# A graph layer on one core: every source row gathered by GpSimd, fewer waits on TensorE, two node blocks a transfer

## The chip, the core and the metric

The kernel runs on one core of a Trainium2 chip. Its time is the device time of the run in microseconds. The core has TensorE (PE; PEld is its weight load), VectorE (DVE), ScalarE (ACT), GpSimd (POOL) and SyncE (SP), which work through their own instruction queues and wait for each other by semaphores. In this kernel POOL, SP and ACT also issue DMAs.

## What is computed

50000 nodes have 160 features: 64 scalars and 32 vectors of three. 1650000 edges, sorted by destination, carry four attributes each. Every edge's message is bilinear in the source node's row and the four attributes; messages are summed per destination, pass a linear layer and a ReLU, and are normalised with two residual additions:

```python
edge_index = jnp.stack([src, dst])
s, v = x[:, :64], x[:, 64:].reshape(n, 32, 3)
ss, vv = s[src], v[src]
e0, e1 = sh[:, 0:1], sh[:, 1:4]
dot  = jnp.einsum('eui,ei->eu', vv, e1)
out0 = C0 * (ss * e0 @ W1 + dot * INV3 @ W2)
p3   = (ss @ W3)[:, :, None] * e1[:, None, :] * INV3
p4   = jnp.einsum('eui,uw->ewi', vv * e0[:, :, None], W4) * INV3
p5   = jnp.einsum('eui,uw->ewi', jnp.cross(vv, e1[:, None, :]), W5) * INV6
out1 = C1 * (p3 + p4 + p5)
m_agg = segment_sum(concat(out0, out1), dst)
h     = concat(m_agg_s @ Ws * LIN_S, m_agg_v @ Wv * LIN_V)
x     = layernorm(x + (x + relu(h)))
```

The last 50000 edges made by the setup are self loops, one per node; after the sort each stands among the edges of its node.

## The kernel before

**Edges.** Since the message is linear in the source row, rows are summed first and multiplied by weights afterwards. Edges are taken 128 at a time (a unit); six units (G) make a group whose destinations fall in a window of 32 nodes (W); two groups make a pair (PG = 2), which is the step of the main loop, 1044 pairs in all. For each unit of a pair POOL gathers 128 rows of x by an indirect DMA into one slice of the tile `xg` (line 319, `gather`). Four `xg` buffers exist (pool "rows"), so POOL can fill the next pairs while PE reads an older one. VectorE makes the one-hot of the destinations (`hot`, line 328) and multiplies it by the four attributes (`ha`, line 331, `spread`); PE multiplies `ha` by the gathered rows and adds up six units in PSUM (`ps`, line 343, `group_sums`; two buffers); VectorE transposes the sums (line 349). Every two pairs make a chunk of four groups. Its sums are multiplied by the weights (`phc`, line 579, `apply_weights`) and copied to SBUF by ScalarE (`hp`, line 581).

**Rows fetched singly.** `HELP = {ET.SP: 72}`: once in 72 units the rows of one unit are not gathered by POOL. SP reads 128 offsets from `ro` (made by ScalarE, line 274) and issues one DMA per row into the tile `xr` (lines 671 to 677, `fetch`, in four batches of 32 over the pairs before). That unit is the last of its pair, and POOL then issues 11 gathers for the pair in place of 12.

**Nodes.** Blocks of 128 nodes (391) follow behind the chunks that they need. `ahead` (lines 588 to 597) issues the DMAs for a block's own rows `xt` and self-loop attributes `sa`; `own` turns `xt` by TensorE (`ptx`, line 615), has ScalarE copy it (`xT`, line 617), multiplies it by the weights (`yx`, line 623) and adds the four products on VectorE into `t` (lines 627, 629); `block` sums the chunks into the nodes (`phb`, line 639) and adds `t` (line 640); `norm1` (184 to 188), `norm2` (line 193, ScalarE) and `norm3` (197, 199) normalise; `do_send` issues the DMA to the output (line 735).

**Packs.** The self loops are taken out of the edge list on the chip beforehand. Rows of 790 edges are worked on 128 at a time (16 packs, each due every 65.8 pairs or so): read (lines 419 to 423), cast by ScalarE (427 to 429), scanned and shifted by VectorE in strides of 1 to 16 (`shift`, lines 504 to 511), and written by SP to the tables `edges` and `selves` row by row (`store`, `put`, line 563). A pack is a list of small steps, some of them empty; the main loop runs as many steps after each pair as spread the list evenly up to the pair at which the pack is due.

**Order.** The main loop calls these parts in the order of the pairs, with `after_pair(p, ...)` for what belongs behind pair p. A scheduler arranges the instructions of PE, VectorE, ScalarE and POOL from that; within the main loop SP keeps the program's order (line 799). Semaphore waits come from a dependency tracker, except for the one that is set by hand: the first product of a pair waits for all of the pair's gathers (lines 346 to 348).

Of the kernel before, what the change touches and what calls it, by code (L numbers as in the profile page):

```python
# [38 lines left out]
F32 = mybir.dt.float32  # L39
# [6 lines left out]
ET = mybir.EngineType  # L46
# [3 lines left out]
P = 128  # L50
MUL0, MUL1 = 64, 32
D = MUL0 + 3 * MUL1
NK = 4
# [9 lines left out]
W = 32  # L63
QG = P // W
FB = P // NK
ND = D // FB
PG = 2
SG = 20

HELP = {ET.SP: 72}  # L70
HEAD = 100
RP = 128
RS = 16
KM = 31
# [29 lines left out]
def tile_gnn_resnorm(ctx: ExitStack, tc: tile.TileContext, x, src, dst, attr, W1, W2, W3, W4, W5, Ws, Wv, out, n_edges):  # L104
# [86 lines left out]
    def norm2(pool, mv, n):  # L191
        rstd = pool.tile([P, 1], F32, name="rstd")
        nc.scalar.activation(rstd[:n], mv[:n, 1:2], AF.Sqrt, bias=eps_t[:n])  # L193
        return rstd

    def norm3(pool, y, mv, rstd, n):
        nc.vector.reciprocal(rstd[:n], rstd[:n])
        o = pool.tile([P, D], F32, name="o")
        nc.vector.tensor_scalar(o[:n], y[:n], mv[:n, 0:1], rstd[:n], op0=ALU.subtract, op1=ALU.mult)  # L199
        return o  # L200

# [23 lines left out]
    with tc.tile_pool(name="once", bufs=1) as once, tc.tile_pool(name="raw", bufs=2) as rawp, \  # L225
# [1 line left out]
            tc.tile_pool(name="far", bufs=3) as farp, \  # L227
            tc.tile_pool(name="ops", bufs=3) as op, tc.tile_pool(name="sums", bufs=4) as sump, \
            tc.tile_pool(name="hp", bufs=alive + 4) as hpp, tc.tile_pool(name="node", bufs=3) as np_, \
            tc.tile_pool(name="ahead", bufs=7) as aheadp, \  # L230
# [93 lines left out]
        def spread(placed, u, n):  # L324
# [8 lines left out]
                                    .to_broadcast([P, n, NK, W]), op=ALU.mult)  # L333
            return ha

        def group_sums(p, rows, ha, at, i):


            s, g0, ng = pairs[p]
            ps = psA.tile([P, PG, D], F32, name="ps")  # L340
            rows, got = rows
            for j, xr in enumerate(rows):
                mm = nc.tensor.matmul(ps[:, j // G, :], ha[:, j].rearrange("p k w -> p (k w)"), xr,  # L343
                                      start=j % G == 0, stop=j % G == G - 1)

                if j == 0 and p + 1 < len(pairs):
                    for r in got[1:]:
                        tc.add_manual_dep(mm.ins, r.name, LANDED)
            nc.vector.transpose(at[:, :, i:i + ng, :].rearrange("p b g w -> p g b w"),  # L349
                                ps[:, :ng].rearrange("p g (b f) -> p g b f", f=FB))  # L350
# [57 lines left out]
        def pack(c):  # L408
# [160 lines left out]


            for head, j in [(False, j) for j in range(RS)] + [(True, 0)]:
                steps += [partial(store, head, j), None, None, None]
            return steps + [stored]

        def apply_weights(at, ng):

            ph = psM.tile([P, D], F32, name="phc", tag="misc")
            for b in range(ND):
                nc.tensor.matmul(ph[:ng * W], at[:, b, :ng].rearrange("p g w -> p (g w)"), BWk[:, b, :], start=b == 0, stop=b == ND - 1)  # L579
            hp = hpp.tile([P, D], F32, name="hp")  # L580
            evict(hp[:ng * W], ph[:ng * W])  # L581
            return hp, ng * W

        def rows_of(b):
            nb = min(P, N - b * P)
            return nb, slice(b * P, b * P + nb)

        def ahead(b):

            nb, row = rows_of(b)  # L590
            xt = aheadp.tile([P, D], F32, name="xt")
            dq.dma_start(xt[:nb], x[row, :])

            assert rows_stored[0] == NR or row_start(rows_stored[0])[1][0] >= row.stop
            sa = aheadp.tile([P, NK], F32, name="sa")
            dq.dma_start(sa[:nb], selves[0, row.start * NK:row.stop * NK].rearrange("(n k) -> n k", k=NK))
            return xt, sa

        def nodes(b):

# [5 lines left out]
                                    rr[:, :len(cs)].unsqueeze(2).to_broadcast([P, len(cs), P]), op=ALU.is_equal)  # L606
            return hot2

        def own(b, xt, sa):

            nb, row = rows_of(b)
            H = D // 2
            pt = psM.tile([H, 2, P], F32, name="ptx", tag="misc")
            for i in range(2):
                nc.tensor.transpose(pt[:, i, :nb], xt[:nb, i * H:(i + 1) * H], ident[:nb, :nb])  # L615
            xT = np_.tile([H, 2, P], F32, name="xT")
            evict(xT[:, :, :nb], pt[:, :, :nb])  # L617
            t = aheadp.tile([P, D], F32, name="t")
            for h in range(NK // 2):
                y = psM.tile([P, 2, D], F32, name="yx", tag="misc")  # L620
                ks = slice(2 * h, 2 * h + 2)
                for i in range(2):
                    nc.tensor.matmul(y[:nb], xT[:, i, :nb], BWh[:, i, ks, :], start=i == 0, stop=i == 1)  # L623
                for i in range(2):
                    k = 2 * h + i
                    if k == 0:
                        nc.vector.tensor_scalar(t[:nb], y[:nb, i], sa[:nb, 0:1], None, op0=ALU.mult)  # L627
                    else:
                        nc.vector.scalar_tensor_tensor(t[:nb], y[:nb, i], sa[:nb, k:k + 1], t[:nb],  # L629
                                                       op0=ALU.mult, op1=ALU.add)  # L630
            return xt, t

        def block(b, xt, t, hot2):
            nb, row = rows_of(b)
            cs = of_block[b]
            ph = psM.tile([P, D], F32, name="phb", tag="misc")
            for i, c in enumerate(cs):
                hp, r = hps[c]
                nc.tensor.matmul(ph[:nb], hot2[:r, i, :nb], hp[:r], start=i == 0, stop=i == len(cs) - 1)  # L639
# [8 lines left out]
        for h, (eng, period) in enumerate(HELP.items()):  # L648
            first = PG * G + h * period // 2
            nbatch = P // ROWS[eng]  # L650
            while True:
                at = [int(first + i * period / nbatch) // (PG * G) for i in range(nbatch)]
                q = at[-1] + 2
                if q >= len(pairs) or pairs[q][2] < PG:
# [50 lines left out]

        later = {}

        def after_pair(p, f, *args):
            later.setdefault(p, []).append((f, args))

# [5 lines left out]
                of_nodes[b] += (nodes(b),)  # L716

        def do_ahead(b):
            of_nodes[b] = ahead(b)

        def do_own(b):
            of_nodes[b] = own(b, *of_nodes.pop(b))
# [5 lines left out]
            rstds[b] = norm2(np_, resid[b][1], rows_of(b)[0])  # L728

        def do_store(b):  # L730
            outs[b] = norm3(np_, *resid.pop(b), rstds.pop(b), rows_of(b)[0])

        def do_send(b):
            nb, row = rows_of(b)
            dq.dma_start(out[row, :], outs.pop(b)[:nb])

        def do_cast(s):
            raws[s] = cast(raws[s])
# [8 lines left out]
        def examine_all():  # L747
# [20 lines left out]
            bad = once.tile([P, 1], F32, name="bad")  # L768
            nc.vector.tensor_reduce(bad, wrong, axis=AX.X, op=ALU.max)
            pb = psM.tile([1, 1], F32, name="pb", tag="misc")  # L770
            nc.tensor.matmul(pb, bad, ones[:, 0:1], start=True, stop=True)
            nc.vector.tensor_scalar(more[:, 0:1], pb, 1.0, None, op0=ALU.min)
            nc.vector.tensor_scalar(more[:, 1:2], pb, 1.0, float(NB), op0=ALU.min, op1=ALU.mult)
# [21 lines left out]
        for at, bs in zip(complete, after):  # L795
            for b in bs:
                after_pair(max(at - AHEAD, START - 1), do_ahead, b)
                after_pair(max(at - AHEAD + 4, START), do_own, b)
        later_pools.enter_context(tc.manual_schedule(engines={ET.SP}))
        for p, (s, g, ng) in enumerate(pairs):  # L800
            if p % per == 0 and s + 1 < NSC:
# [116 lines left out]
    with tc.tile_pool(name="edges2", bufs=2) as ep, tc.tile_pool(name="ops2", bufs=2) as op, \  # L918
            tc.tile_pool(name="node2", bufs=1) as np_, tc.tile_pool(name="psA2", bufs=2, space=PSUM) as psA, \
            tc.tile_pool(name="psF2", bufs=1, space=PSUM) as psF:  # L920
        with tc.For_i(0, blocks, 1) as b:
# [52 lines left out]
            o = norm3(np_, y, mv, norm2(np_, mv, NBLK), NBLK)  # L974
            nc.scalar.dma_start(out[row, :], o[:NBLK])


# [31 lines left out]
```

## Time and profile before

| | |
|---|---|
| median of 5 runs | 15680.33 us (15676.18 to 15682.88) |
| the profiled execution: its own time, its span | 15677.19 us, 15675.4 us |
| busy | POOL 75%, PE 51%, PEld 46%, DVE 40%, ACT 3% |
| PE's granted clock (mean) | 0.739 |
| gathers on POOL (line 319) | 12349 |
| single-row DMAs on SP (line 676) | 22144 |
| HBM traffic over the span | 77 GB/s |

A group line gives engine, operation, what is written and read, the count, then busy time and mean ns of one, and after the second bar the idle time just ahead of the group with what ended it. A line of the waits reads: engine and line, what was waited for, then us in total, how often, and the longest. In the timeline the columns are start and duration in us, then the instruction; in brackets the idle time before it and what ended it. A line of stretches gives, after the window and its length, busy us and count of PE, PEld, DVE, ACT and POOL, then the granted clock, the DMA engines' share and GB/s. A line of the chain gives start, us and what.

### The profile page before, as it was taken

Reading aid. Unit: us, or ns where it says so; the run is one execution under the profiler, and the core shown is the slowest. Engines: PE = TensorE matmul, PEld = TensorE weight load, DVE = VectorE, ACT = ScalarE, POOL = GpSimd, SP = SyncE. Lnnn points to the kernel's source line nnn. Section 1 sums busy time; section 2 is a strip of 40 time slices with the busy share of each in tenths; the row PEclk is TensorE's granted clock in tenths of the full one; section 3 lists DMA queues with packets and bytes.
Section 4 is the critical chain, followed back from the end, with each engine's and each line's share of the span. In section 5 each row is a group of like instructions: output and inputs, shape, how many; then the busy total and the mean of one; then the engine's idle time right before and its main releaser. Section 6 shows DMA issues by size and latency. Waiting matters only on the chain. (4 is left out here: it accounts for less than half of the span.)

```text
span 15675.4 us, 167279 instructions
## 1 busy us (share of the span) xinstructions
PE 7993.0 (51%) x38505; PEld 7261.9 (46%) x38506; DVE 6237.9 (40%) x11070; ACT 537.8 (3%) x1497; POOL 11701.9 (75%) x12363
## 2 busy tenths in 40 slices
PE   4554545555555455454554444555555554555555
PEld 3444444444444444444444444444444444444444
DVE  5342525225253442524435243352433525234322
ACT  0000000000000000000000000000000000000000
POOL 7777777777777777777777777777777777777776
PEclk7777777777777777777777777777777777777777
DMA  3323232232232322323223232322323233232222
GB/s 80 86 73 83 71 79 78 77 85 73 78 80 78 82 73 79 80 78 83 72 79 79 78 82 74 83 73 77 82 76 82 74 79 79 78 80 72 77 73 66
DMA packets 843237, 1218.89 MB, mean 78 GB/s; under 512 B 300227, under 2 KB 623912, under 8 KB 838262
## 3 DMA queue, kind: packets, MB, share of 16 engines
q0 software_dynamic: 592752, 1012.42, 25.1%
q1 hardware_dynamic: 248058, 194.45, 4.3%
q8 instruction: 323, 5.29, 0.1%
q14 instruction: 664, 5.44, 0.1%
q10 hardware_dynamic: 1440, 1.29, 0.0%
HBM read 1135.77 MB, written 71.40 MB: 77 GB/s over the span
## 5 line engine op out<-in xcount | busy, mean ns | idle before, releaser
L319 POOL DMA_INDIRECT xg<-in_x,si x12349 | 11697.7, 947 | 3929.2 <-issue 3714.8
L343 PE MATMUL ps<-xg,ha 128*128 128x160 f32 x24698 | 5301.9, 392 | 6216.4 <-DMA xg<-in_x,si 5311.8
L343 PEld LDWEIGHTS ps<-xg,ha 128*128 128x128 f32 x24698 | 5066.7, 267 | 6439.0 <-issue 5551.3
L349 DVE STREAM_TRANSPOSE sums<-ps 128x320 f32<-128x320 f32 x1044 | 535.4, 513 | 6044.6 <-PE ps L343 5966.1
L331 DVE TENSOR_TENSOR ha<-hot,pk 128x1536 f32<-128x1536 f32 x1044 | 1801.2, 1726 | 722.3 <-PE ps L343 722.2
L579 PE MATMUL phc<-BWk,sums 128*128 128x160 f32 x5220 | 927.0, 331 | 784.7 <-DVE sums L349 678.2
L579 PEld LDWEIGHTS phc<-BWk,sums 128*128 128x128 f32 x5220 | 829.1, 211 | 860.5 <-DVE sums L349 721.1
L623 PE MATMUL yx<-BWh,xT 80*128 80x320 f32 x3128 | 1001.7, 466 | 175.9 <-ACT xT L617 175.0
L627 DVE TENSOR_SCALAR t<-yx,sa 128x160 f32<-128x160 f32 x391 | 149.4, 382 | 1834.6 <-PE yx L623 1824.0
L623 PEld LDWEIGHTS yx<-BWh,xT 80*128 80x128 f32 x3128 | 596.0, 200 | 469.5 <-ACT xT L617 263.0
L639 PE MATMUL phb<-hp,hot 128*128 128x160 f32 x3474 | 605.3, 323 | 300.6 <-DVE t L629 299.8
L639 PEld LDWEIGHTS phb<-hp,hot 128*128 128x128 f32 x3474 | 536.9, 206 | 397.2 <-issue 390.3
L328 DVE TENSOR_TENSOR hot<-bank,rel 128x384 f32<-128x384 f32 x1044 | 553.9, 545 | 4.0
L629 DVE SCALAR_TENSOR_TENSOR t<-yx,sa,t 128x160 f32<-128x160 f32 x1173 | 447.9, 382 | 133.0 <-PE yx L623 107.1
L617 ACT COPY xT<-ptx 80x256 f32<-80x256 f32 x391 | 143.8, 368 | 10391.6 <-PE ptx L615 10083.4
L511 DVE COPY_PREDICATED prow<-marks,prow 128x2370 f32<-128x2370 int32 (+8 forms) x160 | 443.4, 2771 | 0.6
L511 DVE COPY_PREDICATED pra<-marks,pra 128x1580 f32<-128x1580 int32 (+8 forms) x160 | 304.8, 1905 | 0.0
L605 DVE TENSOR_TENSOR hot<-bank,rr 128x512 f32<-128x512 f32 (+2 forms) x391 | 287.9, 736 | 0.0
L640 DVE TENSOR_TENSOR phb<-phb,t 128x160 f32<-128x160 f32 x391 | 129.6, 332 | 360.2 <-PE phb L639 357.6
L581 ACT COPY hp<-phc 128x160 f32<-128x160 f32 x522 | 150.2, 288 | 2909.7 <-PE phc L579 2853.8
L193 ACT ACTIVATE rstd<-mv,eps_t 128x1 f32<-128x1 f32 x391 | 115.2, 295 | 1734.1 <-DVE mv L188 1696.1
L615 PE MATMUL ptx<-ident,xt 128*80 128x128 f32 (+1 forms) x782 | 158.9, 287 | 0.0
(148 smaller groups left out, 2848.9 us busy)
## 6 DMA issues: line engine op xcount, KB each, us to landing
xr<-in_x SPq DMA_DIRECT2D x22144, 0.6 KB
xg<-in_x,si POOLq DMA_INDIRECT x12349
edges<-prow SPq DMA_DIRECT2D x1994, 18.5 KB
r<-edges SPq DMA_DIRECT2D x99, 360.0 KB
selves<-mine SPq DMA_DIRECT2D x1992, 0.5 KB
xt<-in_x SPq DMA_DIRECT2D x390, 80.0 KB
out<-o SPq DMA_DIRECT2D x390, 80.0 KB
pra<-in_attr SPq DMA_DIRECT2D x15, 1580.0 KB
```

The lines of the kernel that those rows point to most:

```text
L319: got.append(nc.gpsimd.indirect_dma_start(out=xg[:, j, :], out_offset=None, in_=x, in_offset=bass.IndirectOffsetOnAxis(ap=placed[0][:, u + ...
L328: nc.vector.tensor_tensor(hot[:, :n], slotsP[:, 0:W].unsqueeze(1).to_broadcast([P, n, W]), rel[:, u:u + n].unsqueeze(2).to_broadcast([P, n ...
L331: nc.vector.tensor_tensor(ha[:, :n], hot[:, :n].unsqueeze(2).to_broadcast([P, n, NK, W]), pk[:, :, u:u + n].rearrange("p k u -> p u k").un ...
L343: mm = nc.tensor.matmul(ps[:, j // G, :], ha[:, j].rearrange("p k w -> p (k w)"), xr, start=j % G == 0, stop=j % G == G - 1)
L349: nc.vector.transpose(at[:, :, i:i + ng, :].rearrange("p b g w -> p g b w"), ps[:, :ng].rearrange("p g (b f) -> p g b f", f=FB))
L511: nc.vector.copy_predicated(what[:n, a:e], mi[:, r].unsqueeze(2).to_broadcast([n, e - a, what.shape[2]]), what[:n, a + d:e + d])
L579: nc.tensor.matmul(ph[:ng * W], at[:, b, :ng].rearrange("p g w -> p (g w)"), BWk[:, b, :], start=b == 0, stop=b == ND - 1)
L605: nc.vector.tensor_tensor(hot2[:, :len(cs)], slotsP.unsqueeze(1).to_broadcast([P, len(cs), P]), rr[:, :len(cs)].unsqueeze(2).to_broadcast( ...
L615: nc.tensor.transpose(pt[:, i, :nb], xt[:nb, i * H:(i + 1) * H], ident[:nb, :nb])
L623: nc.tensor.matmul(y[:nb], xT[:, i, :nb], BWh[:, i, ks, :], start=i == 0, stop=i == 1)
L629: nc.vector.scalar_tensor_tensor(t[:nb], y[:nb, i], sa[:nb, k:k + 1], t[:nb], op0=ALU.mult, op1=ALU.add)
L639: nc.tensor.matmul(ph[:nb], hot2[:r, i, :nb], hp[:r], start=i == 0, stop=i == len(cs) - 1)
```

## The change

- `HELP` is empty: nothing is fetched singly, POOL gathers all units. ScalarE's offsets (`ro`) are no longer made.
- `wrote` and `fresh` keep a list of the PE instructions that wrote each PSUM slot of the tags "misc" and "ps". A write to a slot that two later ones have followed is declared independent of the slot's earlier writers on PE.
- `made` collects ScalarE's copies (`hp`, `xT`) by pair; the first product of pair p waits for those of pair p - 1.
- `own` is divided: `turned` (transposes of `xt` and the copy) is called three pairs after `ahead`, `own` five pairs after; before, all of it was called four pairs after.
- Two neighbouring blocks share one DMA for `xt`, one for `sa` and one for the output (`BP = 2`, `together`). Pool "ahead" has five buffers in place of seven, now of two blocks for `xt` and `sa`; `o` has three of two blocks.
- A pack's store steps are no longer followed by three empty ones.

```diff
-HELP = {ET.SP: 72}
+HELP = {}
+BP = 2
@@ group_sums
+        written = {"misc": [], "ps": []}
+        def fresh(kind):
+            written[kind].append([])
+        def wrote(kind, ins):
+            ws = written[kind]
+            for old in ws[-3] if len(ws) > 2 else []:
+                tc.declare_no_dep(ins.ins, old, reason="its reader has waited for it")
+            ws[-1].append(ins.ins)
+            return ins
...
+                if j % G == 0:
+                    wrote("ps", mm)
+                else:
+                    written["ps"][-1].append(mm.ins)
                 if j == 0 and p + 1 < len(pairs):
-                    for r in got[1:]:
+                    for r in got[1:] + made.pop(p - 1, []):
                         tc.add_manual_dep(mm.ins, r.name, LANDED)
@@ pack
             for head, j in [(False, j) for j in range(RS)] + [(True, 0)]:
-                steps += [partial(store, head, j), None, None, None]
+                steps.append(partial(store, head, j))
@@ apply_weights
-            evict(hp[:ng * W], ph[:ng * W])
+            made.setdefault(now[0], []).append(evict(hp[:ng * W], ph[:ng * W]).ins)
@@ ahead
-        def ahead(b):
+        def together(b):
+            bs = list(range(b // BP * BP, min(nblocks, b // BP * BP + BP)))
+            return bs if all(rows_of(i)[0] == P for i in bs) else [b]
+        def ahead(bs):
...
-            xt = aheadp.tile([P, D], F32, name="xt")
-            dq.dma_start(xt[:nb], x[row, :])
+            xt = aheadp.tile([P, BP, D], F32, name="xt")
+            dq.dma_start(xt[:nb, :len(bs)], x[n0:n1, :].rearrange("(h n) d -> n h d", h=len(bs)))
...
@@ own
-        def own(b, xt, sa):
+        def turned(b, xt, sa):
...
+            made.setdefault(now[0], []).append(evict(xT[:, :, :nb], pt[:, :, :nb]).ins)
+            return xt, sa, xT
+        def own(b, xt, sa, xT):
...
@@ do_send
-            dq.dma_start(out[row, :], outs.pop(b)[:nb])
+            bs = together(b)
+            if b == bs[-1]:
+                n0, n1 = rows_of(bs[0])[1].start, rows_of(b)[1].stop
+                dq.dma_start(out[n0:n1, :].rearrange("(h n) d -> n h d", h=len(bs)),
+                             outs.pop(bs[0])[:rows_of(b)[0], :len(bs)])
@@ main loop
-                after_pair(max(at - AHEAD + 4, START), do_own, b)
+                after_pair(max(at - AHEAD + 3, START), do_turned, b)
+                after_pair(max(at - AHEAD + 5, START + 2), do_own, b)
```

More of the change, by code (lines that the diff above doesn't have):

```diff
@@ L194, in norm2, with norm3 @@
         return rstd
-    def norm3(pool, y, mv, rstd, n):
+    def norm3(o, y, mv, rstd, n):
         nc.vector.reciprocal(rstd[:n], rstd[:n])
-        o = pool.tile([P, D], F32, name="o")
         nc.vector.tensor_scalar(o[:n], y[:n], mv[:n, 0:1], rstd[:n], op0=ALU.subtract, op1=ALU.mult)
@@ L229, in tile_gnn_resnorm @@
             tc.tile_pool(name="hp", bufs=alive + 4) as hpp, tc.tile_pool(name="node", bufs=3) as np_, \
-            tc.tile_pool(name="ahead", bufs=7) as aheadp, \
+            tc.tile_pool(name="ahead", bufs=5) as aheadp, tc.tile_pool(name="outs", bufs=3) as outp, \
             tc.tile_pool(name="psC", bufs=1, space=PSUM) as psC, tc.tile_pool(name="psK", bufs=2, space=PSUM) as psK, \
@@ L340, in group_sums @@
             ps = psA.tile([P, PG, D], F32, name="ps")
+            fresh("ps")
             rows, got = rows
@@ L577, in apply_weights @@
             ph = psM.tile([P, D], F32, name="phc", tag="misc")
+            fresh("misc")
             for b in range(ND):
-                nc.tensor.matmul(ph[:ng * W], at[:, b, :ng].rearrange("p g w -> p (g w)"), BWk[:, b, :], start=b == 0, stop=b == ND - 1)
+                wrote("misc", nc.tensor.matmul(ph[:ng * W], at[:, b, :ng].rearrange("p g w -> p (g w)"), BWk[:, b, :],
+                                               start=b == 0, stop=b == ND - 1))
             hp = hpp.tile([P, D], F32, name="hp")
-            evict(hp[:ng * W], ph[:ng * W])
+            made.setdefault(now[0], []).append(evict(hp[:ng * W], ph[:ng * W]).ins)
             return hp, ng * W
@@ L586, in rows_of @@
             return nb, slice(b * P, b * P + nb)
-        def ahead(b):
-            nb, row = rows_of(b)
-            xt = aheadp.tile([P, D], F32, name="xt")
-            dq.dma_start(xt[:nb], x[row, :])
[L594 to L597, printed above, removed]
+        def together(b):
+            bs = list(range(b // BP * BP, min(nblocks, b // BP * BP + BP)))
+            return bs if all(rows_of(i)[0] == P for i in bs) else [b]
+        def ahead(bs):
+            nb = rows_of(bs[0])[0]
+            n0, n1 = rows_of(bs[0])[1].start, rows_of(bs[-1])[1].stop
+            xt = aheadp.tile([P, BP, D], F32, name="xt")
+            dq.dma_start(xt[:nb, :len(bs)], x[n0:n1, :].rearrange("(h n) d -> n h d", h=len(bs)))
+            assert rows_stored[0] == NR or row_start(rows_stored[0])[1][0] >= n1
+            sa = aheadp.tile([P, BP, NK], F32, name="sa")
+            dq.dma_start(sa[:nb, :len(bs)],
+                         selves[0, n0 * NK:n1 * NK].rearrange("(h n k) -> n h k", h=len(bs), k=NK))
+            return [(xt[:, h], sa[:, h]) for h in range(len(bs))]
         def nodes(b):
@@ L607, in nodes @@
             return hot2
-        def own(b, xt, sa):
+        H = D // 2
+        def turned(b, xt, sa):
             nb, row = rows_of(b)
-            H = D // 2
             pt = psM.tile([H, 2, P], F32, name="ptx", tag="misc")
+            fresh("misc")
             for i in range(2):
-                nc.tensor.transpose(pt[:, i, :nb], xt[:nb, i * H:(i + 1) * H], ident[:nb, :nb])
+                wrote("misc", nc.tensor.transpose(pt[:, i, :nb], xt[:nb, i * H:(i + 1) * H], ident[:nb, :nb]))
             xT = np_.tile([H, 2, P], F32, name="xT")
-            evict(xT[:, :, :nb], pt[:, :, :nb])
+            made.setdefault(now[0], []).append(evict(xT[:, :, :nb], pt[:, :, :nb]).ins)
+            return xt, sa, xT
+        def own(b, xt, sa, xT):
+            nb, row = rows_of(b)
             t = aheadp.tile([P, D], F32, name="t")
@@ L620, in own @@
                 y = psM.tile([P, 2, D], F32, name="yx", tag="misc")
+                fresh("misc")
                 ks = slice(2 * h, 2 * h + 2)
                 for i in range(2):
-                    nc.tensor.matmul(y[:nb], xT[:, i, :nb], BWh[:, i, ks, :], start=i == 0, stop=i == 1)
+                    wrote("misc", nc.tensor.matmul(y[:nb], xT[:, i, :nb], BWh[:, i, ks, :], start=i == 0, stop=i == 1))
                 for i in range(2):
@@ L636, in block @@
             ph = psM.tile([P, D], F32, name="phb", tag="misc")
+            fresh("misc")
             for i, c in enumerate(cs):
                 hp, r = hps[c]
-                nc.tensor.matmul(ph[:nb], hot2[:r, i, :nb], hp[:r], start=i == 0, stop=i == len(cs) - 1)
+                wrote("misc", nc.tensor.matmul(ph[:nb], hot2[:r, i, :nb], hp[:r], start=i == 0, stop=i == len(cs) - 1))
             nc.vector.tensor_tensor(ph[:nb], ph[:nb], t[:nb], op=ALU.add)
@@ L653, in tile_gnn_resnorm @@
                 q = at[-1] + 2
-                if q >= len(pairs) or pairs[q][2] < PG:
+                if q >= len(pairs) - 10:
                     break
@@ L706, in tile_gnn_resnorm @@
         later = {}
+        now, made = [0], {}
         def after_pair(p, f, *args):
@@ L718, in do_ahead, with do_turned @@
         def do_ahead(b):
-            of_nodes[b] = ahead(b)
+            bs = together(b)
+            if b == bs[0]:
+                of_nodes.update(zip(bs, ahead(bs)))
+        def do_turned(b):
+            of_nodes[b] = turned(b, *of_nodes.pop(b))
         def do_own(b):
@@ L730, in do_store @@
         def do_store(b):
-            outs[b] = norm3(np_, *resid.pop(b), rstds.pop(b), rows_of(b)[0])
+            bs = together(b)
+            if b == bs[0]:
+                outs[b] = outp.tile([P, BP, D], F32, name="o")
+            norm3(outs[bs[0]][:, b - bs[0]], *resid.pop(b), rstds.pop(b), rows_of(b)[0])
         def do_send(b):
-            nb, row = rows_of(b)
-            dq.dma_start(out[row, :], outs.pop(b)[:nb])
+            bs = together(b)
+            if b == bs[-1]:
+                n0, n1 = rows_of(bs[0])[1].start, rows_of(b)[1].stop
+                dq.dma_start(out[n0:n1, :].rearrange("(h n) d -> n h d", h=len(bs)),
+                             outs.pop(bs[0])[:rows_of(b)[0], :len(bs)])
         def do_cast(s):
@@ L770, in examine_all @@
             pb = psM.tile([1, 1], F32, name="pb", tag="misc")
+            fresh("misc")
             nc.tensor.matmul(pb, bad, ones[:, 0:1], start=True, stop=True)
@@ L797, in tile_gnn_resnorm @@
                 after_pair(max(at - AHEAD, START - 1), do_ahead, b)
-                after_pair(max(at - AHEAD + 4, START), do_own, b)
+                after_pair(max(at - AHEAD + 3, START), do_turned, b)
+                after_pair(max(at - AHEAD + 5, START + 2), do_own, b)
         later_pools.enter_context(tc.manual_schedule(engines={ET.SP}))
         for p, (s, g, ng) in enumerate(pairs):
+            now[0] = p
             if p % per == 0 and s + 1 < NSC:
@@ L973, in tile_gnn_resnorm @@
             y, mv = norm1(np_, ph, xt, NBLK)
-            o = norm3(np_, y, mv, norm2(np_, mv, NBLK), NBLK)
+            o = np_.tile([P, D], F32, name="o")
+            norm3(o, y, mv, norm2(np_, mv, NBLK), NBLK)
             nc.scalar.dma_start(out[row, :], o[:NBLK])
```

## The prediction

> **What bounds the kernel now.** I read the busy line first, then the costliest groups, the waits of each engine, the timeline around the longest waits, stretches by engine, and the chain that ended last.
>
> ```profile
> PE 7993.0 (51%) x38505; PEld 7261.9 (46%) x38506; DVE 6237.9 (40%) x11070; ACT 537.8 (3%) x1497; POOL 11701.9 (75%) x12363
> ...
> L319 POOL DMA_INDIRECT xg<-in_x,si x12349 | 11697.7, 947 | 3929.2 <-issue 3714.8
> L343 PE MATMUL ps<-xg,ha 128*128 128x160 f32 x24698 | 5301.9, 392 | 6216.4 <-DMA xg<-in_x,si 5311.8
> ...
> xr<-in_x SPq DMA_DIRECT2D x22144, 0.6 KB
> ```
>
> POOL does one thing, L319: 947 ns busy and about 304 ns to the next issue, 12349 times. PE spends 5311.8 us waiting for what POOL fetches, so POOL sets the pace. The SP queue fetched another 22144 rows one by one, which is 22144 / 128 = 173 gathers that POOL did not have to issue.
>
> ```profile
> POOL xg L319 <- issue: 3714.8, 12185, 0.6
> POOL xg L319 <- PE ps L343: 160.4, 21, 22.4
> POOL xg L319 <- DMA xg<-in_x,si: 22.9, 61, 1.4
> ```
>
> POOL's own waits are few: 21 times it waited for PE to free a gather buffer. From the start times in the trace, 12311 gaps from gather to gather are undisturbed and average 1.2510 us; the other 37 are longer by 174.0 us together. The account closes: 9.4 to the first gather, 12349 x 1.2510 = 15448.6, 174.0 of stalls, and 43.7 from the last gather's end to the end of the span make 15675.7 against 15675.4. Fourteen of the stalls (149.5 us) come once a pack, from 911 to 13191 us, and a fifteenth (4.6) at 14241. The rest, 20 us, lie in the first 125 us (13.5) and around the read of the last, partial pack at 13980.
>
> The longest one, in the timeline:
>
> ```profile
> 9436.62 2.71 DVE L511 COPY_PREDICATED prow<-marks,prow 128x2322 f32<-128x2322 int32 x1
> 9440.06 2.78 DVE L511 COPY_PREDICATED prow<-marks,prow 128x2370 f32<-128x2370 int32 x1
> 9443.49 2.67 DVE L511 COPY_PREDICATED prow<-marks,prow 128x2274 f32<-128x2274 int32 x1
> 9444.90 0.95 POOL L319 DMA_INDIRECT xg<-in_x,si  x1 [0.30 <-issue]
> 9446.32 0.51 DVE L349 STREAM_TRANSPOSE sums<-ps 128x320 f32<-128x320 f32 x1
> 9459.95 1.74 DVE L331 TENSOR_TENSOR ha<-hot,pk 128x1536 f32<-128x1536 f32 x1
> 9461.75 6.20 PE L343 MATMUL ps<-xg,ha 128*128 128x160 f32 x24 [3.42 <-DVE ha L331]
> 9468.22 0.94 POOL L319 DMA_INDIRECT xg<-in_x,si  x1 [22.37 <-PE ps L343]
> ```
>
> VectorE works through a pile of pack copies (L511 and its companions) before it gets to the transpose (L349) and the one-hot product (L331) that the pairs need; PE starves, and POOL, with four gather buffers, runs three pairs ahead (3 x 12 x 1.251 = 45 us) and stops.
>
> **Part by part.** *Rows no longer fetched singly.* POOL issues 173 gathers more. Price of one: bounded by 0.947 (busy alone) and 1.251 us (cadence). Before and after each of them stands another gather, so I take the cadence: 173 x 1.251 = **+216.4 us**, all on the path. Does the cadence itself depend on SP's fetches or on VectorE? Two stretches say no:
>
> ```profile
> 8030.00:8070.00 40.00, 28.14 (x139) 24.93 (x140) 15.34 (x38) 2.40 (x8) 30.25 (x33) 0.80 0.28 73
> 9400.00:9440.00 40.00, 3.54 (x12) 3.17 (x12) 37.60 (x46) 0.00 (x0) 30.25 (x33) 0.54 0.27 70
> ```
>
> The third column is VectorE, the fifth POOL: 33 gathers and 30.25 us in both. And the 6028 gaps in which SP issued no row average 1250.9 ns, the 4134 with four issues 1251.2: 0.3 ns, over 12522 gathers 4 us. I count nothing, and keep -4 for the range. What SP loses (22144 x 0.32 us of issue, from 10.3 us for 32) and ScalarE's offsets (L274, 0.42 us a time) stand off the path.
>
> The Trainium skill, "DMA: Bandwidth & Descriptors", section "Issuing engines are not separate DMA queues", says that issuing from several engines saves only the issuing sequencer's time, usually small beside the transfer. Here that time is the kernel: DMA engines are 27 to 28% busy in the two stretches while POOL never pauses. By the rule the 173 gathers would be nearly free and the sum would end at about 15507; by the row it ends 216 us higher. I go by the row.
>
> *Pack steps.* A pack's list shrinks from 128 steps to 77, because its 17 store steps lose three empty ones each; the lists are spread over the same pairs (some 66 a pack), so the 55 steps up to the last copy take about 47 pairs in place of 28. What counts is how VectorE's instructions then stand. In the built order of the kernel before, costed with durations of the groups, VectorE's work between two successive L331 exceeds 45 us at 17 places (81.5 at most, 59 pack instructions between), and the fifteen stalls come four pairs (POOL's lead) after fifteen of them; gaps of 37.3 or less have none. In the built order of the changed kernel the largest gap is 23.6 us; two in a row reach 31, four 53 at most, against 60 us in which POOL fetches four pairs. The piles are gone. So I take back the 15 stalls on PE, **-154.0 us** (160.4 less 21 ordinary gaps of 0.304). Bounds: 0, if something else holds PE as long, and -174.0, if every stall of the trace goes.
>
> *PE's own signals.* In the built order PE instructions that wait on PE fall from 1191 to 592. Nothing: PE is idle for half the span, and the pairs wait for gathers. Without that cover each would be worth some tenths (PE's 0.51 to 0.61 us ahead of L623 and L343 after a signal bound it), 599 x 0.6 = 360 us, but of PE's 7.7 ms of idle time.
>
> *Copies waited for once a pair.* The first product of a pair now waits for ScalarE's xT and hp copies made in the pair before; 517 such waits appear. Behind it queue the pair's 12 products, its transpose, then later pairs; POOL feels it only when PE is 45 us late. A copy is 0.29 to 0.37 us, ordinarily done a pair earlier: nothing; bounds 0 and the 154 us of the stalls that it could put back (second rival).
>
> *Two blocks a transfer.* xt, sa and out drop from 391 issues each to 196 on SP, with 160 KB for 80. Out waits for the second block (2.7 pairs, 40 us); five double xt buffers and three double out buffers cover that. Off the path but for the end. Splitting xT from own moves PE's work a pair or so, off the path too.
>
> *The end.* The chain after the last gather:
>
> ```profile
> 15630.78 4.40 DMA xg<-in_x,si
> ...
> 15636.49 2.42 PE yx L623 x8
> ...
> 15642.55 2.42 PE yx L623 x8
> ...
> 15645.58 2.38 PE yx L623 x8
> ...
> 15652.30 4.58 PE phc L579 x20
> ...
> 15663.47 0.36 DVE o L199
> ```
>
> Three blocks' own products, and a pair held back by its SP row, stand between the last gathered product (over at 15635.76) and the last chunk's weights at 15652.30. In the changed built order all yx products come ahead of the last pair, and no SP row is left: 16.5 us less a transpose and its signal, **-16 us**; bounds 0 and -20.
>
> Sum on the profiled execution's own time: 15677.19 + 216.4 - 154.0 - 16 = 15723.6. It is 3.1 under the median of the runs (15680.33; its span 15675.4 has 1.8 around it), so the forecast is **15727 us**, +46 or 0.3% slower. Its own range: 130 to 160 of stalls back and 5 to 20 at the end, 15716 to 15762. What this kernel's measurement can tell from no change is about 0.2%, 31 us.
>
> **The rivals.** *A new wait takes the piles' place.* ScalarE serves its queue in order: a copy that PE now waits for can stand behind rstd, which waits for VectorE (L193, 46.4 us the longest), or behind the pack's casts, which wait for a 2.4 MB read. PE then stops before the pair, not after, and 16 packs can each cost POOL what they cost now. With a quarter of the 154 us kept the sum is +46 + 38 = +85, with half +123, with all +200: 15765 to 15880. For it: the new waits exist, and both sources show in the waits. Against: POOL has 45 us of slack, and with no pile on VectorE rstd is not held up. 0.15.
>
> *No measurable change.* Every stall goes, the first 125 us included, where the largest gap on VectorE in the built order falls from 62.3 to 20.0 us in the first thirty pairs: 216.4 - 174.0 - 20 - 4 = +18, 15698. It decides once 185 of these 198 us come back. Against: the start waits for loads and weights, which the change leaves. 0.12.
>
> *Faster, by POOL's cadence.* Break-even is 46 / 12522 = 3.7 ns a gather; 0.2% faster asks for 6.2 ns (1.2448), time 15649. The only row for it is the 0.3 ns above. 0.03, of which 0.01 stays within 0.2%.
>
> That the change does not do what it says is excluded for the rows (POOL has 173 more in the built order), and half true for PE's signals, which carry no time.
>
> **How the numbers follow.** Forecast 0.70, new wait 0.15, no change 0.12, cadence 0.03. Range 15698 to 15800: it takes in the forecast, the no-change case and the lower third of the new wait, and leaves out 0.13. Faster 0.02, same 0.13 (0.12 and 0.01), slower 0.85.
>
> **What would show it.** Right: L319 x12522 at 947 ns, the gap still 1.251 us; POOL's waits for ps down from 160.4 to under 20 us; the last gather near 15693; the tail near 28 us; no stretch of VectorE over 25 us without an L331. Wrong: a cadence below 1.247; POOL's wait for ps at 80 us or more, with PE's ps waiting for ScalarE (new wait); stalls at the start gone as well (no change).

## The result, and the profile after

The changed kernel takes **15712.14 us** (median of 24 runs, 15709.78 to 15715.94) against 15678.71 us for the kernel before (44 runs, 15673.43 to 15686.55). The ratio is 1.0022 [1.0016, 1.0027]: slower by 33 us, just past the 31 us named as the limit of what can be told. The forecast was 15727. The profiled execution of the changed kernel took 15703.95 us (span 15702.2), 6 us below the lowest of its other runs; between the two profiled executions the difference is +26.8 us, which lies under those 31. The account below explains those 26.8.

The page: the busy line, then the two groups that were shown of before.

```profile
PE 8079.1 (51%) x38505; PEld 7372.6 (47%) x38506; DVE 6036.3 (38%) x11070; ACT 509.2 (3%) x1392; POOL 11857.9 (76%) x12536
...
L319 POOL DMA_INDIRECT xg<-in_x,si x12522 | 11853.7, 947 | 3822.9 <-issue 3770.5
L359 PE MATMUL ps<-xg,ha 128*128 128x160 f32 x25044 | 5528.4, 401 | 6873.3 <-DMA xg<-in_x,si 5744.2
```

POOL has 173 more gathers at the same 947 ns each, and PE now waits 5744.2 us for them, 432 more than before. POOL still sets the pace. Its own waits (what it waited for, us in total, times, longest):

```profile
POOL xg L319 <- issue: 3770.5, 12377, 0.3
POOL xg L319 <- DMA xg<-in_x,si: 20.9, 63, 1.3
POOL xg L319 <- PE phc L600: 8.5, 28, 0.3
```

The line that stood second before, 160.4 us for PE's `ps`, is gone; what these three lines hold is the ordinary gap of 0.3 us and a short wait for a landing now and then. The two stretches shown of before, again:

```profile
8030.00:8070.00 40.00, 17.25 (x88) 15.53 (x89) 10.81 (x21) 0.84 (x3) 30.25 (x33) 0.76 0.31 86
9400.00:9440.00 40.00, 20.06 (x91) 18.35 (x91) 16.62 (x29) 0.59 (x2) 30.25 (x33) 0.79 0.25 66
```

In the second one VectorE (third pair of numbers) was busy for 37.60 us and PE did almost nothing; now VectorE is busy for 16.62 and PE for 20.06. POOL's 33 gathers in 40 us are the same in all four stretches: before, it went on at its own pace beside the pile and was stopped only behind this stretch (the prediction's timeline has the 22.37 us ahead of the gather at 9468.22), by buffers that PE had not freed.

The end, in the chain that ended last:

```profile
15680.51 4.38 DMA xg<-in_x,si
...
15684.93 0.54 PE ps L359 x2
15685.47 0.93 PE phc L600 x6
15686.40 2.13 PE phb L677 x8
15688.53 1.88 PE phc L600 x10
15690.41 1.10 PE phb L677 x8
...
15694.55 0.36 DVE o L199
```

No own product (`yx`) stands between the last gathered product and the last weights any more.

From the start times of the gathers, the account of both profiled executions (us; "stalls" are gaps above 1.4 us, beyond the mean of the undisturbed gaps; the last column is the time from the last gather's end to the end of the span):

| | to the first gather | gathers x mean gap | stalls | of these in the first 130 us | after the last gather | span |
|---|---|---|---|---|---|---|
| before | 9.4 | 12349 x 1.25100 = 15448.6 | 174.0 | 13.6 | 43.7 | 15675.4 |
| after | 9.9 | 12522 x 1.25022 = 15655.3 | 16.6 | 14.1 | 20.7 | 15702.2 |

The terms are 173 x 1.2502 = +216.3 for the gathers, 12349 x -0.00078 = -9.6 for the gap, -157.4 for the stalls, -23.0 at the end and +0.5 at the start: +26.8.

### The profile page after: what moved, and what is told of

It reads as the page before. It is cut to its first block, busy times and chain, and to the rows that moved or that the text cites. A ratio compares the mean times of both kernels' runs of the same rounds, so it can differ in the third digit from the quotient of the medians.

```text
span 15702.2 us, 120241 instructions
## 1 busy us (share of the span) xinstructions
PE 8079.1 (51%) x38505; PEld 7372.6 (47%) x38506; DVE 6036.3 (38%) x11070; ACT 509.2 (3%) x1392; POOL 11857.9 (76%) x12536
## 5 line engine op out<-in xcount | busy, mean ns | idle before, releaser
L319 POOL DMA_INDIRECT xg<-in_x,si x12522 | 11853.7, 947 | 3822.9 <-issue 3770.5
L359 PE MATMUL ps<-xg,ha 128*128 128x160 f32 x25044 | 5528.4, 401 | 6873.3 <-DMA xg<-in_x,si 5744.2
L359 PEld LDWEIGHTS ps<-xg,ha 128*128 128x128 f32 x25044 | 5305.2, 275 | 7165.1 <-issue 6449.8
L331 DVE TENSOR_TENSOR ha<-hot,pk 128x1536 f32<-128x1536 f32 x1044 | 1805.5, 1730 | 0.1
L531 DVE COPY_PREDICATED pra<-marks,pra 128x1580 f32<-128x1580 int32 (+8 forms) x160 | 304.6, 1904 | 0.1
L646 PEld LDWEIGHTS ptx<-ident,xt 128*80 128x80 f32 (+1 forms) x782 | 75.9, 123 | 396.3 <-issue 337.0
L664 DVE TENSOR_SCALAR t<-yx,sa 128x160 f32<-128x160 f32 x391 | 147.3, 377 | 25.3 <-PE yx L660 18.2
```

The source lines that it names most:

```text
L319: got.append(nc.gpsimd.indirect_dma_start(out=xg[:, j, :], out_offset=None, in_=x, in_offset=bass.IndirectOffsetOnAxis(ap=placed[0][:, u + ...
L331: nc.vector.tensor_tensor(ha[:, :n], hot[:, :n].unsqueeze(2).to_broadcast([P, n, NK, W]), pk[:, :, u:u + n].rearrange("p k u -> p u k").un ...
L531: nc.vector.copy_predicated(what[:n, a:e], mi[:, r].unsqueeze(2).to_broadcast([n, e - a, what.shape[2]]), what[:n, a + d:e + d])
L646: wrote("misc", nc.tensor.transpose(pt[:, i, :nb], xt[:nb, i * H:(i + 1) * H], ident[:nb, :nb]))
```

## The experiments

The prediction put the stalls' end down to the part "Pack steps": a shorter list without the empty steps of the stores, and so a VectorE order without piles. The theories of the first two runs are these. **A**: the piles belong to the rows fetched singly; with them in the program the scheduler puts VectorE's pack work in piles, without them it does not. **B**: the rest of the change, the pack steps first of all, takes the piles away. Each kernel is compared with the kernel before on the same chip. "VectorE pile" below is the longest VectorE work between two one-hot products L331 (L331 itself not counted) in the trace, after the first 130 us. In the kernel before it is 75.3 us, with 13 stretches above 45 us; in the changed one 19.5, with none. "Stalls" and "end" are the columns of the account above.

**Only the rows removed.** In the kernel before:

```
-HELP = {ET.SP: 72}
+HELP = {}
```

> The kernel before with one part of the change alone: nothing is fetched singly; pack steps stay padded, TensorE's waits, block transfers and the division of own stay as before. Its built order has no gap on VectorE over 35.6 us. Theory A: +216 for 173 gathers, -10 by the cadence, -154 for the stalls, and the end of the kernel tells how much of its 23 us the SP row made: 15705 to 15730. Theory B (padding makes the piles): stalls stay, about 15885.

Measured: 15705.42 us (15704.03 to 15707.39), 1.0018 [1.0009, 1.0028]. POOL's wait for `ps` is down to four ordinary gaps:

```profile
POOL xg L319 <- issue: 3777.5, 12401, 0.3
...
POOL xg L319 <- PE ps L343: 1.2, 4, 0.3
```

Stalls are 22.8 us, the pile 29.9, the end 18.0. One line of the diff gives the whole result, with the packs' 128 steps left as they were. Theory A holds.

**Only the rows kept.** In the changed kernel:

```
-HELP = {}
+HELP = {ET.SP: 72}
```

> The changed kernel with one part undone: SP fetches the rows of one unit in 72 singly again. In its built order VectorE's piles of pack work between two successive pair products are back (69.8 us the largest, 17 gaps over 49 us), although the pack's store steps stay unpadded. Theory A (the piles come with the fetched rows, and the piles make POOL's stalls): about 172 gathers fewer, -216 us, cadence 0.8 ns longer, +10, and some 100 us of stalls back (30 to 150): about 15606, range 15530 to 15660. Theory B (the prediction's part on pack steps: the stalls went because the store steps lost their empty ones): no stalls, about 15506. Either way faster than both kernels.

Measured: 15719.26 us (15711.57 to 15724.77), 1.0026 [1.0016, 1.0036]. Both theories had expected it faster than both kernels, and it is not. The gathers are 12350, one more than before, since the changed kernel also ends the single rows ten pairs ahead of the last pair; while `HELP` is empty that does nothing. POOL's waits and PE's waits of this kernel say why:

```profile
POOL xg L319 <- PE ps L359: 221.2, 23, 26.1
```

```profile
PE phc L600 <- DVE sums L369: 990.2, 135, 62.5
```

The wait for `ps` is back, larger than before (160.4), and PE waits for VectorE's transpose up to 62.5 us at a time. One such stall in the timeline (start, duration, instruction, and in brackets the idle time before it):

```profile
6479.49 1.88 DVE L531 COPY_PREDICATED pra<-marks,pra 128x1576 f32<-128x1576 int32 x1
...
6534.53 2.86 DVE L531 COPY_PREDICATED prow<-marks,prow 128x2364 f32<-128x2364 int32 x1
...
6538.52 0.51 DVE L369 STREAM_TRANSPOSE sums<-ps 128x320 f32<-128x320 f32 x1
6539.18 3.00 PE L600 MATMUL phc<-BWk,sums 128*128 128x160 f32 x10 [60.09 <-DVE sums L369]
...
6549.62 0.94 POOL L319 DMA_INDIRECT xg<-in_x,si  x1 [26.12 <-PE ps L359]
```

Pack copies from 6479 to 6537, then the transpose that PE has waited for over 60.09 us, then a gather behind 26.12 us of idle time. The longest pile is 65.0 us, with 15 stretches above 45, in a kernel that has the short pack lists. So theory A has the direction, but its size was missed: stalls are 234.0 us against 16.6 in the changed kernel, 217 us back where it had allowed some 100 and at most 150. In the account that is what eats the 172 gathers: -214.4 for them, +217.4 for the stalls, +4.9 at the end.

**The empty steps put back.** In the changed kernel:

```
-                steps.append(partial(store, head, j))
+                steps += [partial(store, head, j), None, None, None]
```

> The changed kernel with the three empty steps put back behind every store step of a pack. The largest gap on VectorE between two pair products in its built order is 27.5 us. If the piles come with the single rows and not with the padding: no wait of POOL for ps, 15712 within 8. If the padding made them (the prediction's part on pack steps): up to 150 us more, about 15860.

Measured: 15739.48 us, 1.0018 [1.0008, 1.0028] (before on that chip: 15713.1). In the profile, taken from its first run (15700.86 us), POOL has no wait for `ps`, stalls are 15.7, the pile 22.4. The empty steps do not make piles. The absolute figure missed because both kernels were slower there (the last section).

**The other parts, one at a time,** each in the changed kernel. The wait for the copies:

```
-                    for r in got[1:] + made.pop(p - 1, []):
+                    for r in got[1:]:
```

> The changed kernel without the wait of a pair's first product for ScalarE's copies of the pair before; TensorE then waits for the copies where they are needed. If these waits lie beside POOL's gathers: 15712 within 8. If they hold TensorE (the prediction's second rival, of which no stall showed): some us less, no more than the 16 us of stalls that are left.

Measured: 15740.62 us, 1.0018 [1.0009, 1.0028].

PE's waits on its own signals:

```
             ws = written[kind]
-            for old in ws[-3] if len(ws) > 2 else []:
-                tc.declare_no_dep(ins.ins, old, reason="its reader has waited for it")
             ws[-1].append(ins.ins)
```

> The changed kernel with TensorE's waits for its own signals at reused PSUM slots put back; the built order of VectorE stays the same. TensorE's waits grow by some hundred; POOL's account stays: 15712 within 8. A rival: TensorE falls behind at the end or at a pile and a few us appear there.

Measured: 15737.84 us, 1.0016 [1.0006, 1.0026].

Two blocks a transfer:

```
-BP = 2
+BP = 1
```

> The changed kernel with one block a transfer (BP = 1). SP issues 585 more DMAs, off the path: 15712 within 8. Only the end could move: the last blocks' output leaves earlier (up to 5 us less) or queues behind other outputs (up to 5 us more).

Measured: 15739.39 us, 1.0018 [1.0008, 1.0027].

The changed kernel has 1.0022, and 1.0018 in its second set of runs; intervals of 0.001 to each side are some 15 us, so the ratios alone would hide a small effect. The accounts are finer: stalls are 17.0 to 18.2 us and the end 18.4 to 20.9 us in all three, against 16.6 and 20.7. What is left of the distance is the gap between gathers, which is longer in these three profiles (the last section). So these parts move no more than some 2 us of stalls or end.

**Rows kept, piles taken away in another way.** If the order is the cause, then VectorE in the program's own order should be free of piles with the rows in place. In the kernel before:

```
-        later_pools.enter_context(tc.manual_schedule(engines={ET.SP}))
+        later_pools.enter_context(tc.manual_schedule(engines={ET.SP, ET.DVE}))
```

> The kernel before, with VectorE's instructions in the program's order in place of the scheduler's; all the rest as it is, SP's 22144 single rows too. The largest gap on VectorE between two pair products in the built order falls from 81.5 to 25.2 us (the second is 16.3). Theory A (POOL's stalls are VectorE's piles and nothing else): the 15 waits go, -154 us, about 15525, range 15510 to 15560. Rival (the stalls come from the pack's transfers or from SP, and the piles only stand beside them): about 15679. Second rival (in program order VectorE stands behind TensorE's products and the pairs fall behind): slower than 15700.

Measured: **15492.47 us** (15492.07 to 15493.34), 0.9883 [0.9866, 0.9899]: 1.2% faster than the kernel before, and below the range that was expected, since the end and the gap had not been counted. POOL's waits in this kernel:

```profile
POOL xg L319 <- issue: 3731.2, 12239, 1.3
POOL xg L319 <- DMA xg<-in_x,si: 19.2, 56, 0.8
POOL xg L319 <- PE phc L579: 4.9, 16, 0.3
```

The 22144 rows are still on SP, POOL issues 12349 gathers, and of the wait for `ps` 0.8 us is left; the pile is 15.3 us. The stalls were VectorE's order, and neither the rows themselves nor the packs' transfers. Against the profile of before the stalls fall by 156.6, the end by 17.8, the gap gives 9.1 and the start 1.7: 185.2.

**The changed kernel with both.** `HELP = {ET.SP: 72}` as above, and VectorE in the program's order:

```
-HELP = {}
+HELP = {ET.SP: 72}
...
-        later_pools.enter_context(tc.manual_schedule(engines={ET.SP}))
+        later_pools.enter_context(tc.manual_schedule(engines={ET.SP, ET.DVE}))
```

> The changed kernel with single rows by SP as before (one unit in 72) and VectorE in the program's order. If a gather on the path costs its cadence and the piles are all that came with the rows: 15712 - 216 + 10 = 15506, and no wait of POOL for ps. If the single rows bring a cost of their own (cadence, the end, TensorE waiting for them): between 15530 and 15600.

Measured: **15492.24 us** (15491.65 to 15493.55), 0.9882 [0.9866, 0.9899]. It is 14 us below what was expected, and equal to the run above, so with the piles gone the other parts of the change are again worth nothing; and it is 220 us below the changed kernel. By the accounts of the traces (spans 15702.2 and 15489.8, a difference of 212.4) that is 215.7 for 172 gathers with their gaps, 0.4 of stalls, 2.2 at the start, and 6.0 the other way at the end (26.7 against 20.7). So a gather on the path costs 1.25 us here. The two kernels differ in VectorE's order too; one in program order without the rows was not run, but the account leaves no room for another price.

**Why the stalls grew in the second experiment.** There the first product of a pair also waits for the copies. Without that wait (`for r in got[1:]:`), the rest as in "Only the rows kept":

```
-                    for r in got[1:] + made.pop(p - 1, []):
+                    for r in got[1:]:
```

> The changed kernel with one unit in 72 fetched singly and without the wait of a pair's first product for ScalarE's copies; the scheduler orders VectorE. With the wait, POOL's stalls on TensorE were 221 us against 160 in the kernel before, though the piles on VectorE were smaller (69.8 against 81.5 us). If the wait ties TensorE more closely to the piles: stalls fall to 150 to 170, ratio to before near 0.998 (the end is 18 us shorter). If the division of own or the longer list does it: stalls stay at 220, ratio near 1.0026.

Measured: 15703.97 us (15701.4 to 15709.72), 1.0019 [1.0009, 1.0028]. POOL's wait:

```profile
POOL xg L319 <- PE ps L359: 218.3, 29, 25.3
```

218.3 for 221.2: the wait for the copies is not the reason. All stalls are 225.6 us for 234.0 with the wait, so it is worth some 8 us of them at most; the ratio lies between the two that were forecast. The pile here is 77.8 us, with 18 stretches above 45; before, there were 13. What in the changed program's order makes the stalls larger than the 160.4 of before is open.

**More rows on SP.** One unit in 48, then one in 40, in the best kernel:

```
-HELP = {ET.SP: 72}
+HELP = {ET.SP: 48}
```

> The changed kernel with VectorE in the program's order and one unit in 48 fetched singly by SP. If a gather costs its cadence and SP keeps up (260 x 128 rows at 0.32 us are 10.7 ms of SP): some 88 gathers fewer than with one in 72, -110 us: 15382, or a ratio to the kernel before of 0.9813 on the same chip. If SP becomes the bound: POOL waits for ps, and the time is above 15440.

Measured: 16073.39 us (16064.84 to 16083.4), 1.0257 [1.0239, 1.0274], where a gain of some 110 us over the best was expected. Three views of this kernel: the chain by engine and the group of products that read the single rows, from the page; and POOL's and SP's waits.

```profile
SPq 28%; POOL 19%; issue 14%; DMA 5%; PE 3%; DVE 2%; ACT 0%; DVEq 0%; ACTq 0%; POOLq 0%
...
L359 PE MATMUL ps<-xr,ha 128*128 128x160 f32 x514 | 165.7, 414 | 1999.9 <-DMA xr<-in_x 1984.7
```

```profile
POOL xg L319 <- PE ps L359: 699.2, 70, 33.5
```

```profile
SPq L785 <- DVE o L199: 116.3, 3, 68.1
```

PE waits 1984.7 us for the single rows, POOL 699.2 for PE, and SP's queue is the largest part of the chain. VectorE has no pile (12.6 us). Against the kernel with one unit in 72, the 85 gathers fewer give their 104 us, and the stalls take 675. SP's wait ahead of the outputs, its slack, is 116.3 us here; with one unit in 72 it is

```profile
SPq L785 <- DVE o L199: 2658.9, 89, 61.9
```

My budget for SP was too small: it had the rows alone. From the trace, 32896 rows at 323 ns from one to the next are 10.6 ms, 1028 loads of 32 offsets at 2.2 us are 2.3 ms, 272 loads for the packs' stores at 1.2 us are 0.3 ms, and 5005 other DMAs at some 0.3 us are 1.5 ms; together 14.7 of 16.06 ms, and register work lies between them. SP's waits come to 0.6 ms in all, against 4.4 ms with one unit in 72.

```
-HELP = {ET.SP: 48}
+HELP = {ET.SP: 40}
```

> The same with one unit in 40 (313 units, 40064 rows, 12.9 ms of SP's issue beside 1.5 ms of stores). If SP still keeps up: 141 gathers fewer than with one in 72, -176 us, ratio 0.977. If SP falls behind, because it also waits in its queue for outputs (3.7 ms in the kernel with one in 72): stalls of POOL on ps that eat the gain, slower than with one in 48.

Measured: 18524.92 us (18522.31 to 18533.11), 1.1818 [1.1798, 1.1838]. PE waits 6539.2 us for single rows and POOL 3245.7 us for PE. This is the second case of the expectation: slower than one in 48. An overloaded helper costs far more here than it saves.

**The changed kernel once more,** unchanged, beside the last ones:

> The changed kernel unchanged, for the comparison on this chip: a ratio of 1.002 to the kernel before. Its cadence from gather to gather tells whether the 1250 ns, or the 1253 ns seen in three of the four kernels of the batch before, belongs to the kernel: if it does, it is 1250.2 as in its first profile; if it belongs to the chip or the session, it follows the other kernels of this batch.

Measured: 15702.98 us (15701.9 to 15706.53), 1.0018 [1.0008, 1.0027], with a gap of 1.25023 us, stalls 17.1 and 19.0 after the last gather. That is +26.8 us, as between the first two profiles. The profile of the changed kernel is repeated to a few us in every term.

| kernel | gathers | stalls | VectorE pile | time | against before |
|---|---|---|---|---|---|
| before | 12349 | 174.0 | 75.3 | 15678.71 | 1 |
| after | 12522 | 16.6 | 19.5 | 15712.14 | 1.0022 |
| before, no single rows | 12522 | 22.8 | 29.9 | 15705.42 | 1.0018 |
| after, single rows | 12350 | 234.0 | 65.0 | 15719.26 | 1.0026 |
| before, VectorE in program order | 12349 | 17.4 | 15.3 | 15492.47 | 0.9883 |
| after, single rows, program order | 12350 | 16.2 | 12.4 | 15492.24 | 0.9882 |

Few gathers and no piles can be had together; the change buys the second with the first.

## Why the prediction was right, and where it was not

**The gathers** were right: +216.4 forecast, +216.3 in the account, confirmed by the 212.4 us between the changed kernel and its version with the rows kept and no piles. The Trainium skill, "DMA: Bandwidth & Descriptors", section "Issuing engines are not separate DMA queues", calls the issuing time that several engines save usually small beside the transfer. Here it sets the pace: 172 gathers cost 1.25 us each.

**The stalls** were right in size: -154.0 forecast, -157.4 measured, and POOL's wait for `ps` is gone where under 20 us was asked for. The longest VectorE work without an L331 is 19.5 us where 25 was the limit. Reading the built order, and not the lists, gave this.

**The cause in the part "Pack steps" was wrong.** It led from the 51 empty steps that the list loses to the order without piles. The experiments part the two: with the empty steps back there is no pile, and with the short lists but the rows kept there are piles of 65.0 us. What makes them is the scheduler's order of VectorE when the single rows are in the program; why the scheduler orders so with the rows there is not shown. The number came out right since the order was read from the finished kernel; as a forecast of what one part alone does, it would have failed. The prediction had counted nothing for the rows but their gathers.

**The end** was mis-sized: -16, with -20 as the far bound, and -23.0 measured. Up to the last `o`, the part that the prediction worked out, it is -18.6 (32.1 us from the last gather's end before, 13.5 after). The work after the last `o` was not counted: it took 11.6 us in the profile before and takes 7.3 after. Of these 4.3 us, 3.2 are POOL's longest `DRAIN`, an instruction at the program's end; the lines give the shortest, median and longest in ns, before and after:

```profile
L1005 POOLq DRAIN  x3: 40/103/4402, 15670.0 to 15675.0; - x3
```

```profile
L1060 POOLq DRAIN  x3: 40/103/1217, 15700.1 to 15701.9; - x3
```

It takes 1.2 us in all seven profiles without single rows, the two with one block a transfer among them, and 4.4 to 4.5 in all five with one unit in 72 (6.2 with one in 48, 2.0 with one in 40). So it goes with the rows and not with the two blocks a transfer; what it waits for is not shown. The forecast gave the own products and the SP row as reasons for the rest. The experiments do not part these: the end is 18.0 us with the rows alone removed and 25.6 in the changed kernel with the rows kept (none in its last ten pairs), and no own product stands in the last chain of either.

**The gap** was counted at 0, with -4 as its bound, and gave -9.6 between these two profiles. It is not a term of the change: kernels with the rows on SP show 1.2502 to 1.2503 as well, so this part of the distance to the forecast is chance. With the stalls' 3.4, the end's 7.0 and 0.5 at the start the other way, it makes up the 19.6 us by which the profiled execution lies below the sum of 15723.6.

**The rivals.** The new wait: it is there, and cheap. PE's waits after the change have

```profile
PE ps L359 <- ACT rstd L194: 84.6, 39, 5.4
```

with 5.4 us the longest (5.5 is the longest of `ps` on anything of ScalarE's), against POOL's lead of 45; without the wait for the copies the stalls are 18.2 us for 16.6. No measurable change needed the stalls of the start to go too; they stay (13.6 before, 14.1 after), yet the medians came to within 2.4 us of the limit of 31, and on the chip of the second set the difference is 26.8. The outcome lies between the forecast and this rival: the 7.0 us of the end and the gap's 9.6, which is no part of the change, brought it there. Faster by the cadence needed 3.7 ns a gather; it was 0.8 between the two profiles.

**Parts counted at nothing** (PE's own signals, the copies waited for once a pair, two blocks a transfer) are nothing that shows: 1.0016 to 1.0018 without one of them against 1.0018 for the changed kernel in its second set of runs, with the same stalls and the same end within some 2 us.

## What to carry to other kernels

Count what the change adds to the engine that sets the pace at that engine's full cadence, and then read the order that was built for the engines which free its buffers: a pile there longer than its lead stops it, and a change that takes work off the pacing engine may bring the pile. Before giving such work back, try to take the pile away by itself; here one engine in program order kept both gains. A helper engine has a budget too, with its loads and register work in it, and past it the loss is steep.

## What was not expected of the hardware

The undisturbed gap between gathers is not one number. It was 1.2501 to 1.2503 us in ten profiles, 1.2510 in that of the kernel before, and 1.2530 to 1.2531 in three taken on one chip. The difference lies in the gather itself: in the undisturbed gaps it is busy for 945.4 to 945.6 ns in the ten, 946.2 in the kernel before and 948.1 to 948.2 in the three, and POOL is then idle for 304.6 to 304.9 ns in all of them. 3 ns x 12522 gathers are 37 us, more than the whole effect of the change. On that chip the kernel before took 15713.1 us (elsewhere 15676 to 15680), and the kernel with the empty steps took 15700.86 in its first run, which is the profiled one with 1.2501, and about 15739 to 15741 in the others. So it changes between executions on one chip, and no run here shows on what it depends; only the comparison with the kernel before on the same chip holds.

SP takes 2.2 us for each load of 32 offsets, nearly seven times the 323 ns from one row to the next, and this is part of what limits how many rows it can fetch.
